# Fixing the order at the end of an attention layer and of the next layer's input sums, and splitting the first matmuls of two LSTM steps by columns

## The chip, the cores and the metric

The kernel runs on one core of a Trainium2 chip. The metric is the time of one execution on the device in microseconds (us), as the median of several runs. All numbers are fp32.

## The reference

The input is x, 128 sequences of 64 nodes with 256 features, and a 64x64 adjacency matrix. Four layers follow one another. Each computes `x = layernorm(x + layer(x, adj))`:

```python
# layer 0: graph attention
e = leaky(s1[:, :, None] + s2[:, None, :]); e = where(adj == 0, -inf, e)
h0 = softmax(e) @ (x @ W)
# layer 1: edge attention, 512 edges, 4 heads
e = einsum('behd,hd->beh', leaky(Xq[:, src] + Xq[:, dst]), a) + log(adj[src, dst])
attn = segment_softmax(e, src); Y = segment_sum(attn * Xv[:, dst], src); h1 = Y @ W_out.T
# layer 2: graph convolution and a two-layer network with batch norm
agg = A_hat @ x; h = relu(batchnorm(agg @ W1.T + b1)); h2 = batchnorm(h @ W2.T + b2)
# layer 3: two graph convolutions, then an LSTM over windows of p = 1, 2, 3, 4 nodes
h = relu(adj @ (x @ Wg0 + bg0)); h = relu(adj @ (h @ Wg1 + bg1))
for p in 1, 2, 3, 4:
    last = lstm_p(h[:, :(64 // p) * p] cut into windows of p)   # last hidden state of each window
    h[:, p-1, 2p-1, ...] = last                                 # written back at each window's last node
```

What matters for the change in the last layer: the LSTM of step length p reads h as the step lengths before it left it, and each writes only one node in p. The columns that step length p-1 doesn't write are known long before those that it writes.

## The kernel before

**Tiles.** The 8192 tokens (128 x 64) are cut into 16 blocks q of 512. Layers 0 and 1 run block by block in a software pipeline. Layer 1 works on supersteps S of two blocks: `l1_softmax`, `l1_sums` and `l1_weights` make the attention weights of both. `l1_weights` (L383 to L407) transposes on TensorE, takes a reciprocal (`rd`, L395) and forms `at` in four pieces (L397) on VectorE (DVE), and writes each piece by an indirect DMA from GpSimd (POOL) into a table in DRAM (L401). All four write the same table, so each waits for the one before to land. A DMA from SyncE reads the table back (L407). Then `v_a` gathers its part on POOL (`am`, L414) and multiplies (L422), `v_b` applies the output projection (L436), adds (L438) and normalises: statistics on DVE (L95, L96), the inverse root on POOL (L86), and the scaling on POOL (L100) that gives `y`. `v_c` multiplies y by the normalised adjacency (L456) into A, the input of layer 2.

**Layer 2.** A block is a pair of 256-column halves; the up projection of a block is done plainly (`up_block`, matmul L751) or, two blocks at once, as a Strassen-like job of seven products (`Seven`, matmul L822). Such a job first needs four sums of its inputs, `tile_sums`: one on DVE and three on POOL (recorded as L116). Each product is followed by a small operation that combines banks (`use`, L832 to L850). A job's last products (its tail) are issued inside the next job or pass. To fill the end of layer 1, where the pipeline runs out, the loop over `fill` takes turns between the last v_a, v_b, v_c and eleven pieces of the up projection. `sums_at` says after which turn the sums of a job's inputs are made. The down projection begins in `first`, a pass over its matmuls (L1010) with the tail of the last up job between.

**LSTM.** The 128 sequences are 8 groups of 16, in 4 pairs; the array H holds a pair's nodes as columns (node by sequence). For step lengths p = 2, 3, 4, step s = 0 computes gates g, i, o plainly: `plain` (L1458) multiplies x of all windows by the weights (L1469), 21 x 16 = 336 columns at p = 3 and 16 x 16 = 256 at p = 4, for each of two groups and two halves of the gate. Later steps use seven products again (L1504, with DVE, ScalarE (ACT) and POOL combining). The last step's output is written back into H (L1434, on DVE), and the next step length's s = 0 waits for it. Six PSUM banks are shared in turn (`lbank`). In all pairs but the last, other work stands in this wait; in the last pair there is nothing left to put there.

**What sets the order.** A scheduler places instructions of an engine by its own estimates, except where the code says `given(do, ...)` (L110):

```python
for e in latest.values():
    order.enter_context(tc.issue_after(e))
r = do(*args, **more)
```

Everything traced under `given` comes after the latest instruction of every engine that was traced under `given` before it. At the end of layer 1, `l1_softmax` and `l1_sums` of the last superstep, and the tile sums, are given; `l1_weights` and the fill loop aren't.

Of the kernel before, what the change touches and what calls it, by code (L numbers as in the profile page):

```python
# [19 lines left out]
N = 64  # L20
# [21 lines left out]
def kernel(ctx: ExitStack, tc: tile.TileContext, i, out):  # L42
# [87 lines left out]
    with ExitStack() as two:  # L130
# [570 lines left out]
        S = NQ // BPS - 1  # L701
        given(l1_softmax, S)
        given(l1_sums, S)
        l1_weights(S)
        ph.close()


# [193 lines left out]
        def tile_sums(b):  # L901

            t2, t3, t4 = rooms[next(rooms_at) % len(rooms)]
            t1 = b(0, 1)
            given(nc.gpsimd.tensor_tensor, t3, b(1, 1), t1, OP.subtract)
            given(nc.vector.tensor_sub, t1, t1, b(0, 0))
            given(nc.gpsimd.tensor_tensor, t2, b(1, 1), t1, OP.subtract)
            given(nc.gpsimd.tensor_tensor, t4, b(1, 0), t2, OP.subtract)
            return [t1, t2, t3, t4]
# [12 lines left out]
        def inputs(q):  # L922
            return lambda k, n: Aq(q + n)[:, k * QT:(k + 1) * QT]
# [14 lines left out]
            return lambda: up_job(q, g, T[q])  # L938

        fill = [one(n) for n in range(7)] + [pair(n, g) for n in (7, 9) for g in range(2)]  # L940
        sums_at = {4: 7, 6: 9}
        for n, (do, q) in enumerate([(v_b, NQ - LAG - 1), (v_c, NQ - LAG - 1)] + [
                (do, q) for q in range(NQ - LAG, NQ) for do in (v_a, v_b, v_c)]):
            do(q, *[False] * (do == v_c))
            fill[n]()
            if n in sums_at:
                T[sums_at[n]] = tile_sums(inputs(sums_at[n]))
# [33 lines left out]
        ends = range(NQ - LAST, NQ, 2)  # L981
        T = {ends[0]: tile_sums(inputs(ends[0]))}
        given(up_block, q)
        T[ends[1]] = tile_sums(inputs(ends[1]))

        def finish(g):
            def done():
# [4 lines left out]
        def relu(q, m):  # L992
            h = hidden(q, m)
            nc.scalar.activation(h, h, AF.Relu, bias=sh1[:, m:m + 1], scale=sc1[:, m:m + 1])

        def early_relus():
            yield
            for q in range(LAST):
                yield
                given(relu, q, 0)  # L1000

        for g in range(2):
            for q in ends:
                last = q == ends[-1]
                up_job(q, g, T[q], finish(g) if last else None, feed=early_relus() if last and g else iter(()),
                       order=given)

        def down(q, m, p_, ks):
            for k in ks:
# [21 lines left out]
        def first(k, feed):  # L1031
            for q in range(LAST):
                for m in range(M2):
                    if k == 0:
                        pz[q, m] = pbank()
                    given(down, q, m, pz[q, m], [k])
                    if k == M1 - 1:
                        given(nc.vector.bn_stats, st2[:, m, q, :], pz[q, m])
                        if m:
                            for n in range(M2):  # L1040
                                given(leave, q, n, pz[q, n])
                    elif k == 0 and m == 0 and q < 3:
                        next(rest, None)
                next(feed, None)

# [111 lines left out]
    def lbank(shape):  # L1157
        return ps.tile([P] + shape, F32, name="l", bufs=6)
# [180 lines left out]
    def gate_of(n):  # L1339
        return "ifgo".index(n), AF.Tanh if n == "g" else AF.Sigmoid  # L1340

    def lstm(pair):
# [36 lines left out]
        for p in range(2, SKIP + 1):  # L1379
# [74 lines left out]
            def tanh(n, tiles, m):  # L1454
                if n == "i":
                    nc.scalar.activation(tiles["g"][m], cell[:, m], AF.Tanh)  # L1456

            def plain(n, r, tiles):  # L1458

                t = tiles[n] = rows()  # L1460
                at, _ = gate_of(n)
                for m in (1, 0):
                    f, b = bias_of(n, m)
                    joint = 2 * nw * GB <= QT
                    banks = lbank([2, nw, GB]) if joint else None
                    for g in range(2):
                        one = banks[:, g] if joint else lbank([nw, GB])
                        for k in range(KD):
                            nc.tensor.matmul(one, w.raw[0][:, k, at, m, :], inp(r, 0, k)[:, g],  # L1469
                                             start=k == 0, stop=k == KD - 1)  # L1470
                        if not joint:
                            nc.scalar.activation(t[m][:, g], one, f, bias=b)
                    if joint:
                        nc.scalar.activation(t[m], banks, f, bias=b)
                for m in (1, 0):
                    finish(n, r, 0, tiles, m)
                    tanh(n, tiles, m)
# [69 lines left out]
            for r in range(len(runs)):  # L1547
                if p > 2:
                    yield "gap", unit
                for s in range(p):  # L1550
                    last = s == p - 1
                    if s == 0:
                        tiles = {}
                        for at, n in enumerate("gio"):
                            if at == 0 and p > 2:
                                given(input_sums, r, 1)
                            given(plain, n, r, tiles)
                            if at == 0 and p == 2:
                                given(input_sums, r, 1)
                            if at < 2:  # L1560
                                yield "at", unit
                                unit += 1
                    else:
                        names = "fgio"
                        for at, n in enumerate(names):
                            G = nxt or Gate(n, r, s, tiles)
                            nxt = None
                            G.product(1)
                            G.product(5)
                            if prev:  # L1570
                                prev.act(1)
                                prev.act(0)
                                prev.after(1)
                                G.product(2)
                                prev.after(0)
                                prev.tanh(1)
                            G.product(6)
                            if n == "o":
                                G.act(0, 0)
                            if prev:  # L1580
                                prev.tanh(0)
                            G.product(7)
                            if at == 0:
                                given(input_sums, r, s + 1)
                                G.product(3)
                                G.product(2)
                                G.product(4)
                            elif at < 3:
                                G.product(4)
                                G.product(3)  # L1590
                            if at < 3:
                                yield "at", unit
                                unit += 1
                            prev = G
                        o = prev
                        prev = None
                        o.act(1, 1)
                        o.product(3)
                        o.act(0, 1)
                        if p == SKIP and last:  # L1600
                            given(output, r, s, 1, o.tiles["o"], o.tiles["g"], (1,))
                        o.product(4)
                        o.act(1, 0)
                        if p < SKIP or not last:
                            given(output, r, s, 0, o.tiles["o"], o.tiles["g"], (0,))

                    if not last:
                        tiles = {}
                        nxt = Gate("f", r, s + 1, tiles)
                        for j in (1, 5, 6, 7, 3, 2):  # L1610
                            given(nxt.part, j, 0)
                    elif p < SKIP:
                        yield "wait", unit + 1
                    if s:
                        if p < SKIP or not last:
                            given(output, r, s, 1, o.tiles["o"], o.tiles["g"], (1,))
                        given(output, r, s, 0, o.tiles["o"], o.tiles["g"], (1,))
                        if p == SKIP and last:
                            given(output, r, s, 0, o.tiles["o"], o.tiles["g"], (0,))
                        given(hidden_sums, s, lambda: output(r, s, 1, o.tiles["o"], o.tiles["g"], (0,)))  # L1620
                    else:
                        given(hidden_sums, s, lambda: None)
                    yield "at", unit
                    unit += 1
                    if not last:
                        yield "gap", unit
# [135 lines left out]
```

## Time and profile before

| | |
|---|---|
| median of 3 runs | 2061.97 us (2060.48 to 2063.09) |
| the profiled execution | 2064.21 us |
| its span, first to last instruction | 2062.3 us |
| mean granted TensorE clock | 0.983 |
| TensorE busy | 1962.4 us (95%) |
| DVE, ACT, POOL busy | 1187.8, 968.4, 810.8 us |
| instructions | 31449 |

In the profile PE is TensorE's matmul, PEld its weight load; an fp32 matmul of the code appears as two records each of PE and PEld. Times in timelines are us from the span's start. In a timeline a row is the start, the length, the engine, the line, the operation, output and inputs, and the number of instructions in a row of like kind; in brackets stand the idle time before it and what ended it. The granted clock is a share of full speed.

### The profile page before, as it was taken

The page shows a single profiled execution, that of the slowest core. Times are in us where ns is not written, and L with a number is a line of the kernel's source. Part 1 is how long each engine was busy: PE and PEld are TensorE (multiplying, and loading weights), DVE is VectorE, ACT ScalarE, POOL GpSimd, SP SyncE. Part 2 cuts the span into 40 slices and gives each one's busy share as a digit, 9 for nine tenths or more (in the row PEclk, how much of TensorE's full clock was granted, in tenths as well). Part 3 has the DMA queues.
Part 4 walks back from the last instruction along what each step waited for, and adds up shares of the span by engine and source line. Part 5 has one row for each costly group of instructions (what it writes and reads, how often), then busy time and mean ns, then how long its engine had stood idle before and what let it go on. Part 6 is the DMA issues. An engine that isn't in the chain of part 4 may idle for free.

```text
span 2062.3 us, 31449 instructions
## 1 busy us (share of the span) xinstructions
PE 1962.4 (95%) x11583; PEld 1374.8 (67%) x11583; DVE 1187.8 (58%) x2683; ACT 968.4 (47%) x1852; POOL 810.8 (39%) x961
## 2 busy tenths in 40 slices
PE   5999999999899999999999999999999999999997
PEld 4666667675454445687678587678587687586675
DVE  7456665564557456574566674466674466443556
ACT  2766667765245633544333644343644343543333
POOL 1123343343435534263445243345343345133254
PEclk8999999999999998999999999999999999999998
DMA  5444343322202026351232532032521032301022
GB/s 137 77 66 65 79 68 63 57 55 34 44 22 60 31 93 252 110 179 52 87 139 62 194 108 87 11 138 62 188 84 77 1 121 69 128 1 77 1 63 70
DMA packets 235960, 170.68 MB, mean 83 GB/s; under 512 B 150560, under 2 KB 213536, under 8 KB 232480
## 3 DMA queue, kind: packets, MB, share of 16 engines
q1 hardware_dynamic: 233952, 166.72, 28.7%
q8 instruction: 91, 1.49, 0.3%
q0 software_dynamic: 1024, 1.05, 0.2%
q10 hardware_dynamic: 832, 0.92, 0.1%
q14 instruction: 61, 0.50, 0.1%
HBM read 107.82 MB, written 60.82 MB: 82 GB/s over the span
## 4 chain that ended last, share of the span: by engine, by line
PE 59%; DVE 9%; POOL 3%; issue 1%; DMA 1%; ACT 1%; SPq 0%; POOLq 0%; DVEq 0%
PE l L1504 27%; PE l L1469 9%; PE l L1361 8%; PE pz L822 4%; PE g L1324 2%; PE pz L751 2%; PE pz L1010 2%; PE g L1312 1%; PE g L1242 1%; DVE cell L1448 1%; DVE gate L1447 1%; DVE ln_st L95 1%; DVE kept L1525 1%; POOL gate L1527 0%; DVE gate L1523 0%
## 5 line engine op out<-in xcount | busy, mean ns | idle before, releaser
L1504 PE MATMUL l<-xs,wx 128*128 128x256 f32 (+1 forms) x896 | 276.8, 399 | 4.9 <-DVE gate L1523 3.9
L1504 PE MATMUL l<-hs,wh 128*128 128x256 f32 (+1 forms) x896 | 275.1, 399 | 3.1 <-DVE hs L1398 3.1
L86 POOL TENSOR_TENSOR ln_rs<-ln_rs,mhalf 128x2 f32<-128x2 f32 (+2 forms) x98 | 83.9, 856 | 437.4 <-DVE ln_rs L98 425.8
L1519 ACT ACTIVATE kept<-l 128x256 f32<-128x256 f32 (+1 forms) x224 | 88.7, 403 | 339.7 <-PE l L1504 338.5
L1504 PE MATMUL l<-H,wx 128*128 128x256 f32 (+1 forms) x672 | 210.2, 401 | 3.4 <-DVE gate L1532 3.4
L1504 PE MATMUL l<-hid,wh 128*128 128x256 f32 (+1 forms) x672 | 208.7, 399 | 0.0
L1504 PEld LDWEIGHTS l<-xs,wx 128*128 128x128 f32 x896 | 168.8, 190 | 49.3 <-POOL st L100 4.1
L1504 PEld LDWEIGHTS l<-hs,wh 128*128 128x128 f32 x896 | 169.3, 190 | 45.5 <-DVE hs L1398 5.7
L1469 PE MATMUL l<-H,wx 128*128 128x256 f32 (+1 forms) x768 | 187.9, 403 | 6.1 <-DVE H L1434 6.1
L1537 ACT ACTIVATE gate<-gate,bias 128x512 f32<-128x512 f32 (+1 forms) x280 | 170.5, 657 | 37.7 <-DVE gate L1528 31.0
L1469 PEld LDWEIGHTS l<-H,wx 128*128 128x128 f32 x768 | 146.8, 193 | 46.3 <-DVE H L1434 10.4
L1361 PE MATMUL l<-H,wih 128*128 128x512 f32 x384 | 167.5, 597 | 0.0
L357 ACT ACTIVATE u<-z 128x1024 f32<-128x1024 f32 x128 | 130.4, 1025 | 63.3 <-PE z L355 62.3
L1504 PEld LDWEIGHTS l<-H,wx 128*128 128x128 f32 x672 | 126.0, 190 | 38.4 <-DVE gate L1532 7.4
L1504 PEld LDWEIGHTS l<-hid,wh 128*128 128x128 f32 x672 | 127.2, 190 | 32.0 <-issue 2.6
L1361 PEld LDWEIGHTS l<-H,wih 128*128 128x128 f32 x384 | 73.3, 192 | 90.1 <-issue 84.1
L1527 POOL TENSOR_TENSOR gate<-gate,kept 128x256 f32<-128x256 f32 (+1 forms) x84 | 65.2, 776 | 159.0 <-DVE kept L1525 159.0
L329 DVE TENSOR_TENSOR qs<-m,qs 64x256 fp32r<-64x256 f32 x128 | 54.0, 422 | 109.6 <-ACT qs L328 107.5
L1402 POOL TENSOR_TENSOR hs<-hid 128x256 f32<-128x256 f32 (+1 forms) x28 | 25.8, 920 | 200.0 <-DVE hid L1431 116.3
L355 PE MATMUL z<-gath_r,qs 128*128 128x512 f32 x256 | 100.0, 477 | 0.3 <-ACT u L357 0.2
L1456 ACT ACTIVATE gate<-cell 128x512 f32<-128x512 f32 (+1 forms) x88 | 58.6, 666 | 82.3 <-DVE cell L1448 59.1
L1521 DVE TENSOR_TENSOR gate<-l,kept 128x256 f32<-128x256 f32 (+1 forms) x112 | 49.0, 438 | 72.1 <-ACT gate L1537 44.1
(336 smaller groups left out, 3828.4 us busy)
## 6 DMA issues: line engine op xcount, KB each, us to landing
wx<-sums SPq DMA_DIRECT2D x9, 2048.0 KB
wh<-sums SPq DMA_DIRECT2D x9, 1792.0 KB
way<-st SPq DMA_DIRECT2D x54, 256.0 KB
st<-way SPq DMA_DIRECT2D x216, 64.0 KB
xin<-in_x SPq DMA_DIRECT2D x16, 512.0 KB
ld<-table SPq DMA_DIRECT2D x16, 512.0 KB
x_dram<-y SPq DMA_DIRECT2D x16, 512.0 KB
x2r<-x_dram SPq DMA_DIRECT2D x32, 256.0 KB
```

Source lines behind the costliest of these rows:

```text
L86: nc.gpsimd.tensor_tensor(dst, dst, mhalf[:, :n], OP.pow)
L329: nc.vector.tensor_sub(qs[ro, s, :], pq[r, :D], qs[r, s, :].bitcast(F32))
L355: nc.tensor.matmul(z[:, k, :], L1[q]["qs"][c][:, s, k * P:(k + 1) * P], gath_r, start=True, stop=True)
L357: nc.scalar.activation(u, z, AF.Relu)
L822: nc.tensor.matmul(self.bank[at], lhs, rhs, start=first and n == 0, stop=n == len(self.terms) - 1, skip_group_check=True)
L1361: nc.tensor.matmul(b, wih1[:, k, mw * P:(mw + 1) * P], Hw[:, k], start=k == 0, stop=k == KD - 1)
L1456: nc.scalar.activation(tiles["g"][m], cell[:, m], AF.Tanh)
L1469: nc.tensor.matmul(one, w.raw[0][:, k, at, m, :], inp(r, 0, k)[:, g], start=k == 0, stop=k == KD - 1)
L1504: nc.tensor.matmul(self.banks[j], lhs, rhs, start=src == 0, stop=src == 1)
L1519: nc.scalar.activation(self.keep(j), b, AF.Copy)
L1527: e.tensor_tensor(t[0][:, 1], t[0][:, 1], k[5], OP.add)
L1537: given(lambda: nc.scalar.activation(dst, dst, f, bias=b))
```

## The change

It has three parts.

At the end of layer 1, `l1_weights` of the last superstep and all of the fill loop's v_a, v_b, v_c are put under `given`, and the sums of the two jobs' inputs are made one turn later (after turns 5 and 7 instead of 4 and 6). In the order of instructions this puts the four table DMAs on POOL directly behind one another, ahead of y of block 12 and of the tile sums.

In layer 2, the second set of tile sums of the last four blocks is no longer made ahead of the first job; a feed of that job makes it, behind the third product that the job issues. In `first`, one step of the tail moves by one matmul pair.

In the last pair of the LSTM, at s = 0 of p = 3 and p = 4, the columns of H are split into those that step length p-1 doesn't write (two parts) and those it does (one part). At p = 3 they have 160, 96 and 80 columns, at p = 4 96, 80 and 80. The matmuls of gate g (both halves) and of the first half of gate i on the two free parts are issued ahead of the gates; the written part follows in `plain`, and later gates do all three parts. TensorE has 6214 matmuls of the code in place of 6118; DVE, ACT, POOL and SyncE have as many instructions as before.

```diff
@@ end of layer 1
         given(l1_softmax, S)
         given(l1_sums, S)
-        l1_weights(S)
+        given(l1_weights, S)
@@ fill loop
-        sums_at = {4: 7, 6: 9}
+        sums_at = {5: 7, 7: 9}
...
-            do(q, *[False] * (do == v_c))
+            given(do, q, *[False] * (do == v_c))
             fill[n]()
@@ layer 2
         given(up_block, q)
-        T[ends[1]] = tile_sums(inputs(ends[1]))
...
+        def second_sums():
+            yield
+            yield
+            T[ends[1]] = tile_sums(inputs(ends[1]))
+
...
-                up_job(q, g, T[q], finish(g) if last else None, feed=early_relus() if last and g else iter(()),
-                       order=given)
+                feed = iter(()) if last != g else early_relus() if g else second_sums()
+                up_job(q, g, T[q], finish(g) if last else None, feed=feed, order=given)
...
-                    elif k == 0 and m == 0 and q < 3:
+                    elif k == 0 and (q, m) in ((0, 1), (1, 0), (1, 1)):
                         next(rest, None)
@@ LSTM
+            begun = {}
+
+            def late_columns(r):
+
+                if pair < NP - 1 or p == 2 or r:
+                    return [slice(0, nw)], []
+                mine, q = range(nw), p - 1
+                wrote = [w for w in mine if w * p % q == q - 1 and w * p < N // q * q and (q > 2 or w * p >= N // 2)]
+                step = wrote[1] - wrote[0]
+                assert wrote == list(range(wrote[0], nw, step))[:len(wrote)]
+                head = wrote[0] // step * step
+                free = [slice(0, head)] * (head > 0) + [slice(head + n, nw, step) for n in range(step)
+                                                        if head + n != wrote[0]]
+                return free, [slice(wrote[0], nw, step)]
+
+            def begin(n, r, ms, parts):
+
+                at, _ = gate_of(n)
+                joint = 2 * nw * GB <= QT
+                for m in ms:
+                    if (n, m) not in begun:
+                        begun[n, m] = lbank([2, nw, GB]) if joint else [lbank([nw, GB]) for g in range(2)]
+                    for g in range(2):
+                        for c in parts:
+                            for k in range(KD):
+                                b = begun[n, m][:, g] if joint else begun[n, m][g]
+                                nc.tensor.matmul(b[:, c], w.raw[0][:, k, at, m, :],
+                                                 inp(r, 0, k)[:, g, c], start=k == 0, stop=k == KD - 1)
+
             def plain(n, r, tiles):
 
                 t = tiles[n] = rows()
-                at, _ = gate_of(n)
+                free, rest = late_columns(r)
                 for m in (1, 0):
                     f, b = bias_of(n, m)
...
+                    begin(n, r, (m,), rest if (n, m) in begun else free + rest)
+                    banks = begun.pop((n, m))
...
+                        free, rest = late_columns(r)
+                        if rest:
+                            given(begin, "g", r, (1, 0), free)
+                            given(begin, "i", r, (1,), free)
                         for at, n in enumerate("gio"):
```

## The prediction

> **What bounds the kernel now.** I read the busy line and the chain on the profile page first, then looked for the places where TensorE stands still.
>
> ```profile
> PE 1962.4 (95%) x11583; PEld 1374.8 (67%) x11583; DVE 1187.8 (58%) x2683; ACT 968.4 (47%) x1852; POOL 810.8 (39%) x961
> ...
> PE l L1504 27%; PE l L1469 9%; PE l L1361 8%; PE pz L822 4%; PE g L1324 2%; PE pz L751 2%; PE pz L1010 2%; PE g L1312 1%; PE g L1242 1%; DVE cell L1448 1%; DVE gate L1447 1%; DVE ln_st L95 1%; DVE kept L1525 1%; POOL gate L1527 0%; DVE gate L1523 0%
> ```
>
> TensorE (PE) is the bound. So the change is worth only what it takes from PE's gaps, from the slow clock after them, or adds to PE's work. Three groups of gaps touch it. The first is at the attention layer's end; PE's timeline and then GpSimd's (POOL):
>
> ```profile
> 536.88 5.31 PE L751 MATMUL pz<-A,w 128*128 128x512 f32 x12
> 545.53 2.33 PE L456 MATMUL m<-aht,y 64*64 64x64 f32 x64 [3.33 <-POOL y L100]
> 547.78 5.87 PE L751 MATMUL pz<-A,w 128*128 128x512 f32 x8
> 553.59 1.16 PE L422 MATMUL m<-am,v 64*64 64x64 f32 x64
> ```
>
> ```profile
> 537.35 1.51 POOL L401 DMA_INDIRECT table<-at,place  x1 [0.17 <-issue]
> ...
> 540.34 0.99 POOL L401 DMA_INDIRECT table<-at,place  x1 [0.16 <-issue]
> ...
> 543.82 1.04 POOL L401 DMA_INDIRECT table<-at,place  x1 [0.19 <-issue]
> 544.92 2.18 POOL L100 TENSOR_SCALAR y<-y,ln_rs 128x256 f32<-128x256 f32 x4
> ```
>
> PE waits 3.33 us for y, which POOL makes only after tile sums and three table transfers. DVE had the input of the power (L86) ready at 540.7. The other two are in the LSTM's last pair, beside an undisturbed group of the same kind (1834.84):
>
> ```profile
> 1834.84 10.52 PE L1469 MATMUL l<-H,wx 128*128 128x256 f32 x48
> ...
> 1872.07 15.62 PE L1469 MATMUL l<-H,wx 128*128 128x336 f32 x48 [2.53 <-DVE H L1434]
> ...
> 1955.12 12.27 PE L1469 MATMUL l<-H,wx 128*128 128x256 f32 x48 [2.73 <-DVE H L1434]
> ```
>
> The busy times by stretch (PE, PEld, DVE, ACT, POOL; then the granted clock) show what follows each gap:
>
> ```profile
> 546.00:550.00 4.00, 4.00 (x62) 2.77 (x56) 0.00 (x0) 1.08 (x2) 2.12 (x4) 0.50 0.37 139
> 1872.00:1876.00 4.00, 3.93 (x9) 2.35 (x10) 1.02 (x4) 0.90 (x2) 3.16 (x4) 0.64 0.96 410
> 1955.00:1959.00 4.00, 3.88 (x10) 3.20 (x11) 1.32 (x4) 0.36 (x1) 2.93 (x4) 0.57 0.00 0
> ```
>
> Each gap is followed by about 3.4 us (twice that at 545) at half clock. So a gap costs itself plus half of the cold time. Clean price of a record: 10.36/48 = 0.2157 us at 256 columns (1834.84 to the next group at 1845.20); the same cadence at 336 columns is 0.2826 where the clock is full. A matmul of the code is two records.
>
> [...] half clock lasts from 1873.15 to 1876.56 and from 1955.07 to 1958.48, 3.41 us each. [...] The trace has 2.1/2.4/3.5 us (minimum, median, maximum) to landing for L401.
>
> **Part A, attention end.** The four table transfers keep their number but now stand on POOL directly behind one another, ahead of the L86 power and of y. Each waits for the landing of the one before, since all write the same table; the trace shows this wait six times for 14.4 us in all. So y goes from behind three transfers with other work between to behind four with nothing between. On the other side, the tile sums (L116: gath, keep, seg, wv, w; about 1.27 each, 6.4 us) leave this place for one much later. In the new order the reciprocal and at (L395, L397) run without the tile sum on DVE between: at's first piece at about 534.6, table transfers at 534.75, 537.75, 540.65, 543.55. The step of 2.9 is 2.16 landing plus 0.72 of issue, the short end of the back-to-back steps in earlier rounds (2.88 to 4.11, mean 3.5). POOL is free at 544.5, the power (1.06) ends at 545.6, y's first piece (0.65) at 546.25, PE starts L456 at 546.3. PE's order has one L751 matmul (0.86) more before the gap, so PE is busy to 543.05 instead of 542.2. The work between 545.53 and L422 is 6.66 us cold (to 552.19) and 1.40 warm, 4.73 warm in all; less the moved 0.86 that is 3.87. From 546.3, cold to 552.19 does 2.95; 0.92 is left: L422 at 553.1 against 553.59. **-0.5.** SP's loads of the table (L407) follow the last landing, about 4 us sooner (546 against 550.02): the gathers of am(14), am(15) get slack.
>
> The moved sums: now the third DVE sum stands after L834 and waits for POOL's lb, itself behind y of the last block. Queued behind it on DVE are L850 and L847, and PE's products 4 and 3 of the last job there wait for those. I get product 3 at 630.25 against 629.31 (+0.9), y(15) ready in time (the 0.75 wait and the stretched L456 at 622, together -1.67 of slack), and the 1.00 us wait for L834 at 644.47 gone since DVE gets past its bias load sooner. Net **-0.1**; if the covers fail, +1 to +2.
>
> **Part B, layer 2.** The second tile sums go from before the first jobs to behind product 5, 3 POOL operations and one DVE operation with several jobs until their use: nothing, covered by those jobs (3.8 us of POOL if the cover is gone). One tail step in the first L1010 pass moves one matmul later. PE waited 0.94 there:
>
> ```profile
> 665.79 1.12 PE L822 MATMUL pz<-w,w 128*128 128x512 f32 x2 [0.94 <-DVE wq L847]
> ```
>
> One L1010 matmul takes 0.86 and now fills it: **-0.9**.
>
> **Part C, last pair.** At p=3 and p=4, 24 matmuls on columns that the step before doesn't write are issued ahead of the wait for H; in return 24 matmuls of 336 columns become 72 (24 of 160, 24 of 96, 24 of 80) and 24 of 256 become 72 (24 of 96, 48 of 80). The early ones read nothing of the late H, and the l banks come free from 1865 to 1871.7 as PE reaches them. They last 12 x 0.272 + 12 x 0.223 = 5.9 us at p=3 and 24 x 0.223 = 5.4 at p=4 (prices below), longer than gaps of 2.53 and 2.73, so both gaps close and the clock should stay full. The price of a short matmul isn't in these rows; the nearest:
>
> ```profile
> 20.73 1.84 PE L526 MATMUL m<-col_r,qs 128*128 128x2 f32 x16
> ```
>
> 16 records of 2 columns, each with its own load of 128x128, start 0.1115 apart (spacing of the records): the load is the floor. Streaming is 0.836 ns per column and record: 0.134 at 160 columns, 0.080 at 96, 0.067 at 80. If loads overlap streaming, a matmul costs 2 x 0.136 = 0.272 at 160 and 2 x 0.1115 = 0.223 at 96 and 80. Low bound: streaming alone (13.56 and 10.36). High bound: load and streaming in turn, 0.49, 0.38, 0.36. I take the overlap, because the 256-column cadence shows no load at all.
> p=3: 24 x 0.272 + 48 x 0.223 = 17.2 from 1869.54; before, L1469 ended at 1869.54 + 2.53 + 15.62, less 0.14 overlap with the next: 18.15. **-0.9.** p=4: 72 x 0.223 = 16.06 from 1952.39 against 15.0. **+1.1.** So the splitting eats what the gap and the cold clock cost.
>
> **Sum.** -0.5 - 0.1 - 0.9 - 0.9 + 1.1 = -1.3. The profiled execution took 2064.21 (span 2062.3, 1.9 around it), so 2062.9. The median of the runs is 2061.97, 2.24 below that execution: **2060.7**. 0.2% (4.1 us) is about what a measurement can tell from no change.
>
> **Rivals.**
> *Gaps close for less (faster).* [...] no cold time follows and L422 is at 546.3 + 3.87 = 550.2, -3.4 instead of -0.5. If y were not late at all it would be 546.9, -6.7. If short matmuls cost less than the load floor (streaming alone), C gains 3.7 + 5.7 more. For: the clock in the trace went cold with 28 to 34% busy windows and not with 44%. Against: L526's floor. Times: 2057.8, 2054.5 and 2051.3.
> *Loads not hidden (slower).* If a load starts only when the short matmul before it ends, part C costs 24 x 0.49 + 48 x 0.38 + 72 x 0.36 = 56 instead of 33.3: about 2083. It decides from some 0.045 us more per matmul over 120 short ones (5.4 us), that is from 0.27 each. For: no row has 80 columns with a fresh load. Against: PEld is busy 67% of the span under a PE busy 95%.
> *The table chain gets longer (slower).* With 4.1 per step y's first piece comes at 549.8, L422 at 554.9 (+1.3); a third cold window adds 1.7; am(15) then loses its slack of 1.6, and the covers of the moved sums another 2. From the first step 1.8, then 1.7, 2 and 1 on top of -1.3: 2067.2.
> *The order at the attention's end doesn't do what it says.* Fixing it leaves y behind the transfers; that is in my sum already, with the gap still there.
>
> **How the numbers follow.** Forecast 0.52 (its own range 2057.5 to 2064); faster rival 0.29; loads not hidden 0.06; longer chain 0.13. A little of the longer chain stays under +0.2%, a little of the forecast is beyond -0.2%, so: faster 0.30, same 0.52, slower 0.18. The low end 2053 leaves out about 0.1 of full cover or streaming price, the high end 2068 leaves out the unhidden loads and a few others.
>
> **What would show it.** A: four L401 with no POOL work between, 2.9 apart, L456 of this block with a wait of about 3.3 on y L100. B: no wait on L847 at the first L1010 pass. C: no wait on H L1434 ahead of L1469 at p=3 and p=4, clock 1.00 there, 17.2 and 16.1 us for the two groups. Short matmuls over 0.27 apart, or new waits on DVE L834/L850 near 625 to 645 of several us, would make the prediction wrong.

## The result, and the profile after

| | before | after |
|---|---|---|
| median of 20 runs each | 2061.51 us (2058.70 to 2063.09) | 2063.86 us (2061.18 to 2066.67) |
| ratio | 1 | 1.0013, 95% interval 1.0006 to 1.0020 |
| the profiled execution, its span | 2064.21, 2062.3 us | 2062.37, 2060.1 us |

The change makes the kernel slower by 2.35 us by the medians, 1.2 to 4.1 by the interval of the ratio. That is 0.2% at most, and the time lies in the predicted range, but the forecast was 1.3 us faster. The two profiled executions differ the other way (-1.84 us), so they can't just be subtracted. The page of the profile after:

```profile
PE 1966.5 (95%) x11775; PEld 1387.8 (67%) x11775; DVE 1186.3 (58%) x2683; ACT 968.4 (47%) x1852; POOL 807.0 (39%) x961
```

TensorE is busy 4 us longer. The attention layer's end, POOL and then PE:

```profile
533.72 1.08 POOL L401 DMA_INDIRECT table<-at,place  x1 [8.56 <-DVE at L397]
537.24 0.96 POOL L401 DMA_INDIRECT table<-at,place  x1 [2.43 <-DVE ln_mv L96]
540.12 0.96 POOL L401 DMA_INDIRECT table<-at,place  x1 [1.93 <-DMA table<-at,place]
542.99 0.96 POOL L401 DMA_INDIRECT table<-at,place  x1 [1.91 <-DMA table<-at,place]
543.98 1.05 POOL L86 TENSOR_TENSOR ln_rs<-ln_rs,mhalf 128x4 f32<-128x4 f32 x1
545.14 2.16 POOL L100 TENSOR_SCALAR y<-y,ln_rs 128x256 f32<-128x256 f32 x4
```

```profile
535.47 6.17 PE L751 MATMUL pz<-A,w 128*128 128x512 f32 x14
545.74 2.31 PE L456 MATMUL m<-aht,y 64*64 64x64 f32 x64 [4.10 <-POOL y L100]
547.98 4.65 PE L751 MATMUL pz<-A,w 128*128 128x512 f32 x6
552.57 1.16 PE L422 MATMUL m<-am,v 64*64 64x64 f32 x64
```

The four transfers stand in a row, y comes behind them, and PE still waits. The LSTM's two groups, and the clock beside them:

```profile
1865.71 17.36 PE L1488 MATMUL l<-H,wx 128*128 128x160 f32 x144
...
1947.66 16.20 PE L1488 MATMUL l<-H,wx 128*128 128x96 f32 x144
```

```profile
1866.00:1870.00 4.00, 4.00 (x35) 4.00 (x34) 3.22 (x10) 1.73 (x4) 0.90 (x1) 1.00 0.92 303
1948.00:1952.00 4.00, 4.00 (x39) 4.00 (x37) 3.73 (x9) 1.63 (x4) 0.58 (x1) 1.00 0.01 2
```

The waits on H are gone, the clock is 1.00, and the groups take what was forecast. Where, then, do the two executions part? Time of after minus before at the same instruction, along the program:

| place (time in before) | after minus before, us | what lies between it and the place above |
|---|---|---|
| 480 | -3.3 | nothing of the change; half-clock windows at the start lie elsewhere |
| 557 | -1.0 | part A, and half clock at 514 to 521 and 528 to 531, which before hasn't there |
| 667 | -1.2 | rest of part A |
| 687 | -2.0 | part B's wait at the first L1010 pass |
| 1869 (end of the work ahead of p = 3) | -3.7 | half clock at 770 to 815, 13.6 us in both, but at other places |
| end of p = 3's group | -4.6 | part C |
| end of p = 4's group | -3.5 | part C |
| end of the span | -2.2 | nothing that the change touches |

The steps of parts B and C are small, as forecast. The +2.3 from 480 to 557 comes from the half clock at 514 to 521, ahead of part A: 2.3 us are lost there by 524, as in part C alone (2.4), which doesn't have part A. The last row wasn't forecast at all: after the p = 4 group the program is the same, but it takes 96.4 us in place of 95.1. DVE's additions L1650 (L1683 in after, other line numbers in other kernels) wait longer there for a transfer. `final` sends each group through DRAM (a write `way<-st`, then four reads `st<-way`) and DVE adds the result. The last of these, before and after, in DVE's timeline:

```profile
2042.05 0.69 DVE L1650 TENSOR_TENSOR x3r<-st,x3r 128x512 f32<-128x512 f32 x1 [0.68 <-DMA st<-way]
```

```profile
2039.92 0.69 DVE L1683 TENSOR_TENSOR x3r<-st,x3r 128x512 f32<-128x512 f32 x1 [1.28 <-DMA st<-way]
```

### The profile page after: what moved, and what is told of

It reads as the page before. It is cut to its first block, busy times and chain, and to the rows that moved or that the text cites. A ratio compares the mean times of both kernels' runs of the same rounds, so it can differ in the third digit from the quotient of the medians.

```text
span 2060.1 us, 31841 instructions
## 1 busy us (share of the span) xinstructions
PE 1966.5 (95%) x11775; PEld 1387.8 (67%) x11775; DVE 1186.3 (58%) x2683; ACT 968.4 (47%) x1852; POOL 807.0 (39%) x961
## 3 DMA queue, kind: packets, MB, share of 16 engines
q8 instruction: 93, 1.52, 0.3%
## 4 chain that ended last, share of the span: by engine, by line
PE 75%; DVE 14%; POOL 4%; ACT 3%; issue 3%; DMA 1%; SPq 0%; DVEq 0%; POOLq 0%; ACTq 0%
PE l L1533 27%; PE l L1488 9%; PE l L1365 8%; PE pz L822 4%; PE e L346 3%; PE m L318 3%; PE pz L751 2%; PE g L1328 2%; PE m L321 2%; PE pz L1014 2%; PE z L355 2%; DVE ln_st L95 1%; PE g L1316 1%; PE m L253 1%; PE g L1246 1%
## 5 line engine op out<-in xcount | busy, mean ns | idle before, releaser
L1533 PE MATMUL l<-H,wx 128*128 128x256 f32 (+1 forms) x672 | 210.3, 401 | 3.4 <-DVE gate L1561 3.4
L1488 PE MATMUL l<-H,wx 128*128 128x256 f32 (+4 forms) x960 | 193.6, 360 | 0.9 <-DVE H L1438 0.9
L1488 PEld LDWEIGHTS l<-H,wx 128*128 128x128 f32 x960 | 160.3, 190 | 33.5 <-issue 4.1
L1533 PEld LDWEIGHTS l<-H,wx 128*128 128x128 f32 x672 | 125.8, 190 | 38.2 <-DVE gate L1561 7.4
```

Source lines behind the costliest of these rows:

```text
L1488: nc.tensor.matmul(b[:, c], w.raw[0][:, k, at, m, :], inp(r, 0, k)[:, g, c], start=k == 0, stop=k == KD - 1)
L1533: nc.tensor.matmul(self.banks[j], lhs, rhs, start=src == 0, stop=src == 1)
```

## The experiments

**Each part alone.** A cold window is a stretch of 3.41 us at half clock; in before's and after's profiles, up to the end of the TensorE work, one to three of them stand in a row. Two theories: that part A costs the time (attention-end theory), or that part C does (phase theory), because the cold window behind a gap comes only in some executions, while the split costs in all.

Part A alone has the diff's first three edits, part B alone the layer 2 edits, part C alone the LSTM edits. The fourth kernel is part C with

```diff
-                    begin(n, r, (m,), rest if (n, m) in begun else free + rest)
+                    begin(n, r, (m,), rest if (n, m) in begun else [slice(0, nw)])
```

> Part A alone (order at the attention's end, later input sums). Phase theory ([...] part A is about neutral): between -0.5 and +1.0 us against before. Attention-end theory (the four table DMAs in a row and the moved sums cost what is seen): +2 to +3 us. The recorded prediction: -0.6 us.

> Part B alone (second input sums inside the first job, tail step one matmul later). Both theories: -0.9 us, the wait of 0.94 us on L847 in the first L1010 pass gone; if it doesn't do that, 0.

> Part C alone (columns). Phase theory: in the executions in which the gap before L1469 is not followed by a cold window, part C costs 17.2 - 16.1 = +1.1 us at p=3 and 16.1 - 13.1 = +3.0 us at p=4; with a cold window behind about half of the gaps it costs +1.5 to +3 us over many runs. Attention-end theory and the recorded prediction: +0.2 us. Both: no wait on H ahead of L1469, clock 1.00, groups of about 17.3 and 16.2 us.

> Part C, but gates issued after H is ready (the second half of i, and o) use whole columns again: 12 matmuls of 336 columns in place of 36 short ones at p=3, 12 of 256 in place of 36 at p=4. If a short matmul costs 0.223 (load floor) and 160 columns 0.272: 12 x (0.718 - 0.565) = 1.8 us less at p=3 and 12 x (0.669 - 0.431) = 2.9 us less at p=4, so 4.7 us less than part C alone. If the extra time of part C isn't in its short matmuls: no difference to part C alone.

| kernel | ratio to before | us | p = 3, p = 4 in its profile |
|---|---|---|---|
| A alone | 0.9995 (0.9987 to 1.0004) | -1.0 | 18.00, 14.88 |
| B alone | 0.9999 (0.9991 to 1.0008) | -0.2 | 17.99, 14.72 |
| C alone | 1.0009 (1.0002 to 1.0016) | +1.9 | 17.04, 15.87 |
| C, later gates whole | 0.9980 (0.9972 to 0.9988) | -4.1 | 15.24, 13.06 |
| before | 1 | 0 | 17.99, 14.84 |

(The last column is the time from the end of the work ahead of the group to the first matmul behind it, the gap included.) Part A alone measured -2.7 to +0.8 us, so the attention-end theory's +2 to +3 falls. Part A's execution ran in step with before's up to 519 us (within 0.06), so these two can be compared: L422 comes at 553.17 against 553.59, and at 667 it is 0.51 us ahead in all. Part B does remove its wait (0.85 us between 667 and 687), but alone it lost 0.8 us between 625 and 655, where PE waited 0.60 us at 641 and 0.82 at 647 in place of 1.00 once; why wasn't tested. Part C slows the kernel, although its groups cost -0.95 and +1.03 in the profile, as predicted. The gaps were followed by half clock in all three profiles that still had them, so "only in some executions" doesn't explain it well either. Whole columns save 4.6 us in the groups (4.7 expected; 6.0 over the runs): the price of short matmuls holds.

**The tail.** What was left was the tail, all that follows the p = 4 group. It took 95.1, 94.8 and 94.7 us in before, A and B, and 95.8, 95.8 and 96.4 us in C, C with whole gates, and after. The trace lists the packets of every DMA queue. Queue 8, of the kind `instruction`, brings packets of 16 KB. They are taken to be TensorE's instructions, some 256 a packet, since the counts fit: 91 packets for 23402 TensorE records in before (257 each), 93 for 23790 in after (256). So they are called fetches here. In these two profiles a packet takes 0.88 to 1.78 us, and in the tail they come 28.5 to 30.6 us apart. In before they came 2.0, 31.5 and 60.6 us after the p = 4 group; in after 14.6, 45.3 and 73.7 us. DVE waits on the round trips at about 13.5 to 21, 41 to 48 and 68 to 75 us. The DMA view of the last one, after (2035 to 2040.5) and before (2038 to 2043.5):

```profile
q1 hardware_dynamic: 724, 0.41, 24.9%
q8 instruction: 1, 0.02, 1.1%
```

```profile
q1 hardware_dynamic: 697, 0.38, 22.5%
```

Part C adds 96 matmuls of the code, or 384 TensorE records, one and a half packets at 256 each. In after the fetches in the tail come 12.6, 13.8 and 13.1 us later than in before, about half a period, and on the three round trips. That can be put to the test without touching the tail: unused matmuls ahead of the first one, where TensorE waits for its input.

```diff
         load_x(1)
+        idle = bank([P])
+        for _ in range(32):
+            nc.tensor.matmul(idle[:64, :64], ident[:64, :64], ident[:64, :64], start=True, stop=True)
```

The third and fourth kernel begin only gate g early and have all else whole (`given(begin, "i", ...)` taken out of the kernel above).

> The changed kernel with 31 unused 64x64 matmuls ahead of the first one (123 more TensorE instructions, while TensorE waits for its first input), so that the places at which TensorE's instructions are fetched (16 KB each, 256 instructions) in the last 100 us move by about half a period, to where they are in the kernel before. Fetch theory (fetches fall on the DRAM round trips way/st of the final stage and make DVE's L1650 late): from the end of the p = 4 group to the end of the span 95.0 us as before in place of 96.4, and about 1 us less than the changed kernel over many runs. Chance theory (those late transfers are chance): about 96, no difference.

> The kernel before with 32 unused 64x64 matmuls ahead of the first one (127 more TensorE instructions): the fetches move to where part C puts them. Fetch theory: the tail grows from 95.0 to about 96 us, waits of DVE for st<-way of 0.5 us and more; +0.5 to +1.3 us over many runs. Chance theory: 95.0, no difference.

> Part C with only gate g begun early (16 short matmuls), everything after H whole. By the prices of the prediction, p = 3: 8 x 0.718 + 16 x 0.565 = 14.8 us from the end of the work before it, against 18.0 before; p = 4: 8 x 0.669 + 16 x 0.431 = 12.2 against 14.8. Sum -5.8 us. Fetch theory: the fetches lie as in part C alone, so about 1 us of it goes in the tail: -4.8. Chance theory: -5.8 on average.

> The same with 32 unused 64x64 matmuls ahead of the first one, which puts the fetches in the tail back to where they are in the kernel before. Fetch theory: tail 95.0 us, -5.8 us in all, about 1 us better than without them. Chance theory: no difference to c_g.

| kernel | ratio to before | us | fetches after the p = 4 group | tail |
|---|---|---|---|---|
| after + 31 | 0.9984 (0.9977 to 0.9991) | -3.3 | 2.1, 31.6, 60.4 | 94.7 |
| before + 32 | 0.9988 (0.9982 to 0.9994) | -2.5 | 16.3, 44.9, 73.9 | 96.6 |
| C, only g early | 0.9984 (0.9978 to 0.9991) | -3.3 | 15.6, 46.6, 74.4 | 97.3 |
| C, only g early, + 32 | 0.9950 (0.9937 to 0.9962) | -10.4 | 2.0, 31.6, 60.4 | 94.8 |

The tails do as the fetch theory says, both ways: the kernel before gets the long tail, the changed kernel the short one. The whole times show that the unused matmuls do more. The changed kernel gained some 6 us by them, where its tail gives 1.7 and 1 was expected, gate g alone gained 7.1 where 1 was expected, and the kernel before became faster although its tail grew. In the profile of before + 32 the program is 4.9 us ahead at 480 us, and its gaps in the LSTM weren't followed by half clock:

```profile
1862.59 13.94 PE L1472 MATMUL l<-H,wx 128*128 128x336 f32 x48 [2.53 <-DVE H L1437]
...
1943.96 11.02 PE L1472 MATMUL l<-H,wx 128*128 128x256 f32 x48 [2.73 <-DVE H L1437]
```

From the work before to the work behind that is 16.30 and 13.58 us, against 17.99 and 14.84 in before. So a gap isn't always followed by a cold window. Gate g alone costs 14.62 and 12.34 us, 5.9 less than before's two groups (5.8 expected); over its runs it gave -3.3 of an expected -4.8, with a tail 2.2 us longer than before's.

**The start.** Three more, with other numbers of unused matmuls:

> The kernel before with 64 unused 64x64 matmuls ahead of the first one (255 more TensorE instructions, so the fetches in the tail lie where they lie in the kernel before). With 32 of them the run was 2.5 us faster than the kernel before although its tail grew by 1.5. Fetch theory: tail 94.7 to 95.1 us, and 1.5 us faster than with 32, so about -4 us against before, the rest of it from the start. If the tail's 1.5 us were due to anything else that the unused matmuls bring: tail 96 or more.

> Part C alone with 32 unused matmuls ahead of the first one (fetches in the tail as in the kernel before). Fetch theory: tail 94.8 us in place of 95.9. Against the kernel before with 64 unused matmuls it shows what part C costs without the fetches: +0.1 us if its gaps are always followed by a cold window, +3.0 if never, so between.

> Parts A and B as in the changed kernel, part C with only gate g begun early and all else whole, and 31 unused matmuls ahead of the first one. Tail 94.8 us. By the sums so far: part C's form -5.8 and the start about -3 (with cold windows, less without), A and B together -1.2: -8 to -11 us. If A and B are worth nothing here, as much as without them (-10.4, from five runs).

| kernel | ratio to before | us | tail |
|---|---|---|---|
| before + 64 | 1.0007 (0.9999 to 1.0015) | +1.4 | 94.8 |
| C alone + 32 | 0.9993 (0.9986 to 1.0000) | -1.4 | 94.6 |
| A, B, and C with only g early, + 31 | 0.9970 (0.9958 to 0.9982) | -6.2 | 94.7 |

The tails are right again, the times aren't: 64 unused matmuls cost 3.9 us against 32, where 1.5 less was expected. C alone + 32 came out 2.8 us faster than before + 64, where 0.1 to 3.0 slower was expected, and the last kernel gave -6.2 of an expected -8 to -11. Whatever is put at the start moves it (at 480 us these profiles are 1.8 to 4.9 us ahead of before's, those without unused matmuls there 0 to 3.6), so these times can't price the fetches. The last kernel is slower than the one without A and B; its profile lost the difference at the start and between 514 and 558 us, in half-clock windows, and the cause wasn't tested further.

**Fetches and edits apart.** TensorE has a pause at 768 us (3.31 us in before and in after, it waits for DVE). Unused matmuls put there move no other instruction in the order of TensorE's, DVE's, ACT's or POOL's work; SyncE issues one (with 31 and 32) or three (with 63 and 64) of its transfers near 770 us at another place in its order:

```diff
     pr = gbank([P])
+    for _ in range(32):
+        nc.tensor.matmul(pr[:64, :64], ident[:64, :64], ident[:64, :64], start=True, stop=True)
```

> The kernel before with 32 unused 64x64 matmuls in TensorE's pause at 768 us (no other instruction moves on any engine): fetches in the tail as in the changed kernel. Fetch theory: tail 96 to 97.3 us in place of 95, 1.5 us slower than with 64 of them. If the edits themselves cost the time: tail 95, no difference between 32 and 64.

> The same with 64: fetches in the tail as in the kernel before. Both: tail about 95 us, as the kernel before, less at most what a warmer clock after the pause at 768 us brings.

> The changed kernel with 31 unused matmuls at that pause: fetches in the tail as in the kernel before. Fetch theory: tail 94.7, and against the kernel before with 64 only what the edits cost: between -1.3 us (cold window behind each gap) and +1.6 us (none). If the edits cost the time: +2.4 us against the kernel before with 64.

> The same with 63: fetches as in the changed kernel. Fetch theory: tail 96.4, 1.5 us slower than with 31. If the edits cost the time: no difference to 31.

| | fetches as in before | fetches as in after |
|---|---|---|
| before | + 64: 1.0015 (1.0008 to 1.0021), tail 94.9 | + 32: 1.0007 (0.9999 to 1.0015), tail 97.1 |
| after | + 31: 1.0001 (0.9993 to 1.0009), tail 94.9 | + 63: 1.0023 (1.0013 to 1.0033), tail 98.0 |

The unused matmuls took 3.83 us for 31 and 7.56 for 63, so the larger number costs up to 3.7 us more. But it stands once in each column and once in each row. At equal numbers, after against before is 1.0023 - 1.0015 = +1.6 us where after has the bad fetches, and 1.0001 - 1.0007 = -1.2 us where before has them. With e for the edits and f for the fetches, e + f = 1.6 and e - f = -1.2: the fetches cost 1.4 us, the edits 0.2, each about 1.7 either way if the four intervals count as independent. They share the runs of before, which cancel here. By the means of the four kernels' own runs the two differences are +2.1 and -1.3, which makes the fetches 1.7 us and the edits 0.4; with every run counted as independent, the intervals are 0.8 to 2.5 and -0.5 to 1.3. By the times alone that leans to the fetches without deciding; the profiles add the place. The last addition in DVE's timeline, of before + 32 and of before + 64:

```profile
2040.47 0.69 DVE L1652 TENSOR_TENSOR x3r<-st,x3r 128x512 f32<-128x512 f32 x1 [1.49 <-DMA st<-way]
```

```profile
2042.06 0.69 DVE L1652 TENSOR_TENSOR x3r<-st,x3r 128x512 f32<-128x512 f32 x1 [0.28 <-DMA st<-way]
```

In the first the wait is 1.49 us, in the second, the same program but for 32 matmuls 1270 us earlier, 0.28. The additions behind three of the round trips are late in the first: counted from the p = 4 group the lag is 1.15 us at the first, 1.58 at the second and 2.84 at the third. A rival would be that TensorE waits for its own instructions. It doesn't in these two profiles: each of its waits of more than 0.1 us in the tail was ended by DVE, and three of them are longer in before + 32, those behind the late additions. The wait behind the first trip, in PE's timelines of before + 32 and of before + 64:

```profile
1990.87 1.14 PE L1506 MATMUL l<-xs,wx 128*128 128x256 f32 x4 [1.33 <-DVE gate L1525]
```

```profile
1994.11 1.14 PE L1506 MATMUL l<-xs,wx 128*128 128x256 f32 x4 [0.45 <-DVE gate L1525]
```

Between 850 and 1860 us, with 42 fetches in each, these four kernels keep their distance to before within 0.1 us. So from 850 us on, the moved fetches cost nothing ahead of the LSTM's last groups.

Over all 17 profiles: ten kernels with fetches at about 2 us (before or behind), 30 to 32 and 60 to 61 us behind the p = 4 group have tails of 94.6 to 95.1 us (mean 94.8); six with them at 14 to 17, 44 to 47 and 73 to 75 have 95.8 to 98.0 (mean 96.9). The two don't overlap, and both sets hold kernels with part C and without it, and with A and without. The seventeenth, C with later gates whole, has 95.8 as well and shows the place best. It adds half as many instructions, its fetches come at 5.0, 35.9 and 68.9 us, and only the third of them meets a round trip. Its first two additions come at 20.72 and 48.35 us, as in the ten (20.68 to 20.75 and 48.33 to 48.42), and its third at 75.49, late (74.37 to 74.82 in the ten):

```profile
2035.35 0.69 DVE L1679 TENSOR_TENSOR x3r<-st,x3r 128x512 f32<-128x512 f32 x1 [1.38 <-DMA st<-way]
```

**Part A over all profiles.** Six of the profiles have part A, eleven don't. The wait of L456 for y is 3.6 to 4.4 us in the six, and in all six two cold windows (6.8 us) begin about its end. In the eleven it is 1.95 to 3.35 us; three of them, before among them, have two cold windows there, five have one and three have none. The two ends, after and before + 32 (the one of the last table), in busy times by stretch (the third number from the end is the granted clock):

```profile
545.00:551.00 6.00, 5.26 (x68) 3.54 (x69) 0.00 (x0) 1.09 (x2) 4.07 (x6) 0.50 0.29 99
```

```profile
545.00:551.00 6.00, 5.77 (x112) 3.10 (x106) 0.69 (x1) 2.34 (x4) 2.28 (x4) 1.00 0.32 105
```

From 524 to 600 us, against the same stretch of before, the six take 0.8 us less to 0.1 more (mean -0.3), the eleven 0 to 2.1 less (mean -1.3). So by the profiles part A costs about 1 us here on average, and before's own execution was the dearest of those without it. This is a comparison of profiles that differ in other edits too, one execution of each. The runs of part A alone (-1.0, between -2.7 and +0.8) don't show such a cost, so it stays a likely cause, not a shown one.

## Why the prediction was wrong in sign, step by step

- **Part A.** Transfers about 2.9 apart, y still late, PE waiting: right (2.88, 2.87, the first step 3.52; wait 4.10 for 3.25). L456 was forecast for 546.3, L422 for 553.1; in A's own profile, in step with before, they came at 546.43 and 553.17. The stalls behind the late tile sums were found where they were put (1.00 us on L850 at 624.88, 1.32 us at 630.09), and the wait at 644 went. Forecast -0.6, seen -0.51 in this pair. That agreement is in part luck: both executions had two cold windows at this gap. Over all profiles the part costs about +1.0 instead of -0.5, since without it the gap is often followed by one cold window or none.
- **Part B.** Forecast -0.9, seen -0.85 in after. The cover of the moved sums held there; alone, the part lost it again 20 us earlier.
- **Part C, price.** 72 matmuls at p = 4 took 1963.70 - 1947.66 = 16.04 us, 0.2228 each; forecast 0.223. That is 0.1114 a record of 80 or 96 columns, beside 0.1115 a record of 2 columns at L526; that the load sets this floor is the author's reading of the two. p = 3 and p = 4 forecast -0.9 and +1.1, seen -0.95 and +1.03. The rival that loads aren't hidden (0.36 to 0.49 each) is refuted, and so is streaming alone (0.134 to 0.161).
- **Cold windows.** "Each gap is followed by about 3.4 us at half clock" was one execution's answer. It held at p = 3 in six of seven profiles with the gap (17.99 to 18.00 us), and once not (16.30 us). Where it doesn't hold, part C costs 17.03 - 16.30 + 15.87 - 13.58 = +3.0 instead of +0.1; at one in seven this adds some 0.4 us, an estimate from seven profiles of different kernels. Nor does a busy share between 34 and 44% part cold from warm, as one rival's argument had it: in before's own profile full stretches of 3.41 us that were 47 and 48% busy (1.60 us from 808.19, 1.65 from 50.43) were followed by half clock, and one of 45% (1.52 us from 528.30) wasn't.
- **The step that failed** is the sum: it ended at the p = 4 group and counted part C's added instructions only by TensorE's time. They came with two more packets of queue 8 (93 for 91), and with the packets behind them moved the tail was 1.3 us longer in after's profile (2.1 on average of the kernels above). -1.3 + 2.1 + 0.4 = +1.2 us, the lower end of what was measured. A second step is likely: the sum took the half clock behind the gap of part A from one execution, one of the dear ones. With +1.0 for part A in place of -0.5 it comes to +2.7, beside the 2.35 measured (1.2 to 4.1); the four kernels of the last set give +1.6. The tail's share rests on experiments, part A's on the comparison of profiles alone, and how the 2.35 divide between them stays open.
- **The slower rivals** named the wrong mechanisms: the loads are hidden (0.2228 us a short matmul, where unhidden ones were put at 0.36 to 0.49), and the table chain has steps of 2.9 us (the first 3.5), not 4.1. The faster rival through a gap without cold window was the wrong way round, for part C and for part A: it makes the kernel before faster, shown by the clock for part C, by the comparison of profiles for part A.

A version that beats both is part C with gate g alone begun early and 32 unused matmuls at the start: 2050.78 us (five runs) against 2061.23, ratio 0.9950 (0.9937 to 0.9962). Without the unused matmuls the same is 0.9984 (0.9978 to 0.9991), and that part is the sounder, since it follows from 5.9 us saved in the two groups, less 2.2 lost in the tail.

## What to carry to other kernels

Split a matmul by columns only where the wait really is: the later gates, whose input was long there, paid 4.6 us for nothing. Price an edit that adds instructions also by the packets of the instruction queue, and look where those land among transfers that somebody waits for (tails of 96.9 us on average where they met the round trips, 94.8 where they didn't). Don't price a gap by the half clock that followed it in one execution: the same gap of 2.53 us had it in before (17.99 us with the group) and not in before with 32 unused matmuls at the start (16.30). And a difference of two profiled executions is worth nothing below the spread of their half-clock windows (here some 5 us); pair profiles that run in step up to the edit, or compare a stretch by its own ends.

## What the runs showed of the hardware

Queue 8, of the kind `instruction`, is visible DMA work: 91 packets in before, 93 in after, 16 KB each, 0.88 to 1.78 us long. A round trip of 256 KB through DRAM on which one fell was late nearly always. `final` has six such trips, the first about at the end of the p = 4 group. In the sixth and last of them the time from the issue of the last read to DVE's addition was 2.94 to 3.38 us in the six kernels whose fetch falls there, and 2.02 to 2.15 in the ten whose fetch doesn't; in the second, the write took 3.94 to 5.03 us in five of the six and 3.17 to 3.49 in the ten. The exception is before with 32 unused matmuls at the start (3.40), whose first fetch came latest of the six, at 16.3 us. In C with later gates whole it is the sixth trip's write that meets the fetch: 4.29 us, against 3.18 to 3.64 in the ten. How the packets get into each other's way isn't shown.

And the same gap of 2.53 us, ahead of p = 3, cost 4.4 us in before and 2.7 in before with 32 unused matmuls at the start: the group took 17.99 and 16.30 us, where 48 records at 0.2826 take 13.56. In the traces of before and after the times between two changes of the clock are multiples of 3.41 us, up to the last change (1 to 310 times in before, 1 to 362 in after). Counted in such steps, the gap of before lay in one step, which left it busy for 1.08 of 3.41 us, and half clock followed. In the other two steps of this length share the gap; they were busy for 2.60 and 1.70 us, and full clock went on. Whether this is why isn't shown by one pair. The steps of before and then of the other (the first busy time is PE's):

```profile
1869.74:1873.15 3.41, 1.08 (x4) 0.61 (x5) 3.19 (x9) 1.65 (x4) 0.39 (x1) 1.00 0.89 308
```

```profile
1857.46:1860.88 3.42, 2.60 (x13) 1.95 (x11) 3.21 (x8) 1.66 (x3) 0.00 (x0) 1.00 0.32 57
1860.88:1864.29 3.41, 1.70 (x6) 1.05 (x7) 2.66 (x8) 1.31 (x3) 1.00 (x2) 1.00 0.77 308
```
